# Score blocks without their masked quarter in a fused attention and FFN block, short tiles with their rows swapped

## The chip, the cores and the metric

One core of a Trainium2 chip. The metric is the device time of one execution in microseconds. TensorE (PE) does the matmuls, VectorE (DVE) reductions and elementwise work, ScalarE (ACT) activations and copies, GpSimd (POOL) elementwise work in SBUF, SyncE (SP) issues nearly all the DMAs.

## What is computed

The input x is 8 batches of 1024 rows of 256 numbers, fp32 throughout. The first half is causal self-attention with 16 heads of 64 and a bias that depends on the distance of key and query:

```python
bias = rel_table[clip(pos[None, :] - pos[:, None] + 16, 0, 32)]   # per head
q, k, v = x @ Wq, x @ Wk, x @ Wv                                   # per head, 64 columns
scores = q @ k.T / 8 + bias
scores = where(tril, scores, -inf)
out = softmax(scores) @ v
y = x + layernorm(concat(out) @ Wp + bp)     # x was normalised before q, k, v
```

The second half is a feed-forward block on the normalised y (a mix with the row before, a sigmoid gate, a squared relu), with a normalised residual again. Every distance of 16 or more into the past has the same bias, which softmax takes away; so the kernel adds the bias only in a band of 144 columns that ends with a tile's diagonal block, and sets the masked scores there to -1e30.

## The kernel before

**Units and tiles.** The work is cut in 64 units: 8 batches by 8 pairs of heads. The two heads of a pair lie on partitions 0-63 and 64-127 of q and k. A unit has 8 tiles of scores, tile tb being 128 queries (tb*128 on) against the (tb+1)*128 keys that they may see. Tiles 0 to 3 are *short* (128 to 512 keys), tiles 4 to 7 *long* (640 to 1024 keys). A unit goes in four steps, each with a long and a short tile: (7, 1), (6, 0), (5, 3), (4, 2) (STEPS, L21).

**A score tile, do_scores (L974).** A long tile is computed in two parts of half its keys, each in a PSUM tile "s" of two banks (ring "sl" of two, allocated from a pool, L411); the diagonal block is at the end of the second part. A short tile is one part, in two of four fixed PSUM banks "pm" (L377) that all other matmuls use too. A part is four matmuls (L1000): two query halves (output partitions 0-63 and 64-127) by two heads (contraction over partitions 0-63 and 64-127), each of 64x64 weights against all the part's keys. In the diagonal block, the first query half against the second 64 keys is wholly masked, and is computed all the same. Then, for the part that has the diagonal, DVE adds the band table bm (L1029); bm is one SBUF tile of 128 x 16 heads x 144. DVE takes the maximum (nmax, L1037), ACT the exponential into SBUF with its sum (p, L1057), POOL scales by the reciprocal sum (L1145).

**After it.** turn (L1156) transposes p in blocks of 32x32 on DVE (L1166), shuffle (L1219) moves the blocks to their partitions with 16 DMAs (L1226), and do_av (L1234, matmuls at L1252) multiplies by v into pm, two heads in the two column groups. save (L1269) copies the result to oT. project_out (L651) multiplies oT by Wp. Projections q, k, v (do_qk, do_v), project_out and the FFN use the helper matmul (L388), which splits the 128 output partitions in two matmuls of 64; their array shape is 128 rows by 64 columns, where the scores' is 64 by 64. Each fp32 matmul makes two records in the profile.

**The order of the work.** Every piece is a task that is handed to a Planner (L128) with an engine, an estimated cost, what it reads and writes, and a priority. The planner simulates the engines (L191) and writes each engine's instructions out in the order of the better of two simulations (run, L278). Matmul tasks have a mode: "rows" for scores, "cols" for all others. A change of mode is charged SWITCH = 0.09 us, and a task in the other mode has URGENT added to its rank when PE picks its next task (L216). RANK (L46) adds an offset per kind of task to the first simulation's priorities. The start of the kernel, up to the first tiles, is planned alone, without RANK (L1393). The band table is made at the start: a line per head is written to DRAM (skew, L1336) and read back skewed to bm (L1340).

Of the kernel before, what the change touches and what calls it, by code (L numbers as in the profile page):

```python
# [42 lines left out]
URGENT = 1.05  # L43
# [3 lines left out]
    "pe:part.go": -0.82,  # L47
    "dve:top.go": 1.9,
    "act:exp.go": -3.14,
    "dve:bias.go": 1.02,  # L50
    "pool:do_scores.behind": 6.53,
    "act:do_scores.<lambda>": -2.87,
    "pool:do_scores.both": 6.86,
    "dve:do_scores.<lambda>": -0.11,
    "pool:do_scores.<lambda>": -4.38,
    "pool:scale.go": 6.48,
    "dve:one.go": 1.8,
    "pe:do_qk.go": -0.33,
    "act:do_qk.<lambda>": -20.88,
    "sp:shuffle.move": 21.5,  # L60
    "pe:do_v.go": 0.57,
    "act:do_v.<lambda>": 11.6,
    "sp:load_wqk.go": -9.79,
    "sp:load_wv.go": 1.65,
    "pe:do_av.go": 0.22,
    "act:save.<lambda>": -6.41,
    "sp:load_rows.<lambda>": -6.4,
    "dve:norm_stats.go": 2.38,
    "pe:one.go": -0.19,
    "dve:one.plus_old": -14.51,  # L70
    "pool:normed.power": -0.11,
    "pool:normed.go": 6.49,
    "dve:by_dma.<lambda>": -1.51,
    "sp:by_dma.leave": -24.02,
    "sp:by_dma.<lambda>": -17.77,
    "act:by_dma.place": 4.69,
    "pool:plus.go": -26.3,
    "pool:s2.<lambda>": -47.14,
    "act:s3.go": 2.12,
    "dve:s4.go": 3.56,  # L80
    "pe:s5.go": 0.53,
    "act:s5.<lambda>": 17.56,
    "pool:s5.<lambda>": -0.97,
    "pe:second.go": -2.43,
    "act:s6.<lambda>": 22.56,
    "dve:s7.<lambda>": -5.69,
    "sp:s9.<lambda>": -14.9,
    "pe:some.go": 1.42,
    "act:normed.go_edge": -15,
# [18 lines left out]
class Ring:  # L108


    def __init__(self, pool, shape, tag, n):
        self.pool, self.shape, self.tag, self.n, self.owners = pool, shape, tag, n, []

# [14 lines left out]
class Planner:  # L128
# [149 lines left out]
    def run(self, rounds, urgent=1.0, rank={}):  # L278
# [25 lines left out]
        for t, _, _, seen in order:  # L304
            t.held = held.get(t, ())
            for b in t.makes:
                b.tile = b.ring.pool.tile(
                    b.ring.shape, F32, tag=b.ring.tag, name=b.name, bufs=b.ring.n
                )
                if b.view is not None:  # L310
                    b.tile = b.view(b.tile)
            t.fn()
            t.seen = seen
# [3 lines left out]
def tile_attn_ffn_block(  # L317
# [59 lines left out]
    bank = [ps_m.tile([P, HB], F32, name=f"pm{i}") for i in range(4)]  # L377
    plan = Planner(len(bank))
# [9 lines left out]
    def matmul(dst, lhs, rhs, first, last):  # L388
# [20 lines left out]
        "k": Ring(acts, [P, T], "k", 2),  # L409
        "v": Ring(acts, [P, NT, P], "v", 1),  # L410
        "sl": Ring(ps_l, [P, 2, HB], "sl", 2),  # L411
# [33 lines left out]
    def load_wqk(u, prio):  # L445

        pr = units[u][1]
        for name, w in (("q", Wq), ("k", Wk)):
            buf = weights[u, name] = R["w" + name](f"w{name}_{u}")

            def go(buf=buf, w=w):
                for cc in range(NC):
                    nc.sync.dma_start(
                        buf.tile[:, cc, :].rearrange("p (h d) -> p h d", d=D),
                        w[2 * pr : 2 * pr + 2, cc * P : (cc + 1) * P, :].rearrange(
                            "h p d -> p h d"
                        ),
                    )

            add("sp", 2 * ISSUE, go, w=[buf], prio=prio)  # L460

# [189 lines left out]
    def project_out(b, c, prs, prio):  # L651
# [6 lines left out]
        def one(k):  # L658
            def go():
                for pr in prs:  # L660
                    matmul(
                        pm(t)[:, :C],
                        oT[b, pr, c].tile[:, (1 - k) * P : (2 - k) * P],
                        wp_sb[:, pr, :],
                        (pr == prs[0]),
                        (pr == prs[-1]),
                    )
# [306 lines left out]
    def do_scores(u, tb, prio):  # L974


        n = (tb + 1) * P
        size = "long" if n > HB else "short"
        parts = [(0, n // 2), (n // 2, n)] if n > HB else [(0, n)]
# [7 lines left out]
        def part(i, c0, c1):  # L987

            sl = R["sl"](f"s_{what}_{i}") if size == "long" else None
            keep = [sl] if sl else []  # L990

# [3 lines left out]
            def go():  # L995
                for half in range(2):
                    for hh in range(2):
                        rows = slice(hh * D, (hh + 1) * D)
                        o = half * D
                        nc.tensor.matmul(  # L1000
                            s(hh)[o : o + D],
                            q.tile[rows, tb * P + o : tb * P + o + D],
                            k.tile[rows, c0:c1],
# [6 lines left out]
                0.05 + (c1 - c0) * 0.00169,  # L1010
# [11 lines left out]
            def bias(h0, h1):  # L1022
                def go():
                    if sl:
                        dst = sl.tile[:, :, c1 - c0 - w : c1 - c0]
                        src = bm[:, 2 * pr : 2 * pr + 2, BW - w :]
                    else:
                        dst, src = s(h0)[:, n - w : n], bm[:, 2 * pr + h0, BW - w :]
# [3 lines left out]
                done = add("dve", cost, go, t, bm_done, r=keep, prio=prio - 0.5)  # L1032
# [268 lines left out]
    with tc.tile_pool(name="prep", bufs=1) as prep:  # L1301
# [38 lines left out]
        bm_done = add("sp", ISSUE, lambda: nc.sync.dma_start(bm, moved), skew_done, prio=-4)  # L1340
        load_wv(0, -3)
# [21 lines left out]
        load_wqk(1, -1)  # L1363
        for half in range(2):
# [64 lines left out]
    for m in range(LAST):  # L1429
# [10 lines left out]
        if st == 3:  # L1440
            if u + 2 < NU:
                load_wqk(u + 2, m)
            do_v(u, 1, m + 0.3)
# [70 lines left out]
```

## Time and profile before

| | |
|---|---|
| median of 3 runs (lowest, highest) | 2208.03 us (2206.36, 2208.11) |
| profiled execution, its own time | 2206.46 us |
| its span, first to last instruction | 2204.7 us |
| granted TensorE clock, mean | 0.997 |
| ACT busy, POOL busy | 1412.6 us, 1524.2 us |
| PE and DVE busy from 30 to 2100 us | 2061.52 us, 1886.13 us |
| PE waits for another engine or a DMA, whole span | 22.3 us in 11 waits, 9.6 of them ahead of its first matmuls |
| DMA queue of SyncE | 272,144 packets, 384.87 MB, 72.1% of the 16 DMA engines' time |
| 1 shuffle DMA (d from blocks, 2032 of them) | 144 KB, 2.6 us from issue to landing |

Busy times are summed per engine over the execution; engines work side by side, so they do not add up to the span. A line of the timeline gives start, length, engine, source line, operation, output and inputs, shape and count. A matmul's start is recorded, and its end is modelled, so the lengths of neighbouring matmuls overlap; distances between starts are what can be trusted. "64*64" and "128*64" are the rows and columns of the array in use.

### The profile page before, as it was taken

How to read it: one execution, taken by the hardware profiler on the slowest of the kernel's cores; microseconds unless marked ns; L12 is line 12 of the kernel's file. 1: busy time of each engine (PE TensorE's matmuls, PEld its weight loads, DVE VectorE, ACT ScalarE, POOL GpSimd, SP SyncE). 2: the span in 40 equal slices, each digit the busy share in tenths (PEclk: the TensorE clock that was granted, in tenths of full speed). 3: DMA queues.
4: the chain of work that ended last, by engine and by line, in shares of the span. 5: the costliest groups of instructions: out<-in, count | busy, mean ns of one | idle time of the engine just before them, and what ended most of it. 6: DMA issues, size and time to landing. Idle time of an engine off the chain costs nothing.

```text
span 2204.7 us, 61232 instructions
## 1 busy us (share of the span) xinstructions
PE 2172.5 (99%) x21312; PEld 1175.2 (53%) x21312; DVE 1967.5 (89%) x4460; ACT 1412.6 (64%) x4314; POOL 1524.2 (69%) x3709
## 2 busy tenths in 40 slices
PE   7999999999999999999999999999999999999997
PEld 3455555555555545555555555555555555555565
DVE  5989999989999899998999889999898989999876
ACT  5666766657576676766667566666666656666554
POOL 4666677766777667776677757776677866677553
PEclk9999999999999999999999999999999999999999
DMA  5878877778777887777877787777777768777560
GB/s 159 188 179 204 197 176 173 173 192 194 184 168 174 195 192 173 173 172 194 190 177 173 168 205 191 176 173 170 196 186 174 180 167 214 180 183 180 128 160 25
DMA packets 272596, 388.92 MB, mean 176 GB/s; under 512 B 142624, under 2 KB 199968, under 8 KB 272160
## 3 DMA queue, kind: packets, MB, share of 16 engines
q1 hardware_dynamic: 272144, 384.87, 72.1%
q8 instruction: 170, 2.79, 0.5%
q14 instruction: 138, 1.13, 0.2%
q10 hardware_dynamic: 144, 0.14, 0.0%
HBM read 59.91 MB, written 25.29 MB: 39 GB/s over the span
## 4 chain that ended last, share of the span: by engine, by line
PE 92%; DVE 4%; DMA 1%; POOL 1%; ACT 1%; issue 0%; SPq 0%; ACTq 0%; DVEq 0%; POOLq 0%
PE pm L392 47%; PE pm L1252 22%; PE s L1000 16%; PE pm L1000 7%; DVE nmax L1037 1%; DVE blocks L1166 1%; DMA out_dram<-r 1%; DMA skew<-line 0%; DMA raw<-in_L_ffn_W_r_dram 0%; POOL p L1145 0%; ACT p L1057 0%; DVE pm L1029 0%; DVE xk L801 0%; DVE s L1029 0%; DMA tab<-in_L_attn_rel_table_dram 0%
## 5 line engine op out<-in xcount | busy, mean ns | idle before, releaser
L1145 POOL TENSOR_SCALAR p<-p,rcp 128x512 f32<-128x512 f32 (+5 forms) x1536 | 882.9, 591 | 108.7 <-DVE rcp L1124 77.1
L1057 ACT ACTIVATE p<-s,nmax 128x512 f32<-128x512 f32 (+3 forms) x1024 | 618.9, 607 | 416.2 <-DVE nmax L1037 320.2
L1166 DVE STREAM_TRANSPOSE blocks<-p 128x256 f32<-128x256 f32 (+1 forms) x1016 | 733.1, 754 | 46.1 <-POOL p L1145 38.3
L1037 DVE TENSOR_REDUCE nmax<-s 128x2 f32<-128x1024 f32 (+3 forms) x512 | 519.8, 1015 | 22.0 <-PE s L1000 18.1
L1252 PE MATMUL pm<-d,v 128*64 128x256 f32 (+1 forms) x5120 | 523.4, 359 | 0.0
L1252 PEld LDWEIGHTS pm<-d,v 128*64 128x64 f32 x5120 | 351.8, 137 | 217.9 <-issue 36.8
L1000 PE MATMUL s<-k,q 64*64 64x512 f32 (+3 forms) x4096 | 415.9, 517 | 5.6 <-ACT p L1057 5.4
L1057 ACT ACTIVATE p<-pm,nmax 128x256 f32<-128x256 f32 (+3 forms) x512 | 267.6, 525 | 144.2 <-DVE nmax L1037 104.1
L1000 PEld LDWEIGHTS s<-k,q 64*64 64x64 f32 x4096 | 142.4, 132 | 215.3 <-issue 98.4
L392 PE MATMUL pm<-wv,xnT 128*64 128x128 f32 x4096 | 248.0, 274 | 0.0
L392 PE MATMUL pm<-xnT,wq 128*64 128x512 f32 x1024 | 243.9, 597 | 2.6 <-ACT p L1057 2.6
L392 PEld LDWEIGHTS pm<-wv,xnT 128*64 128x64 f32 x4096 | 226.6, 137 | 36.6 <-ACT p L1057 14.1
L392 PE MATMUL pm<-xnT,wk 128*64 128x512 f32 x1024 | 245.2, 600 | 0.0
L392 PE MATMUL pm<-wp_sb,oT 128*64 128x256 f32 x2048 | 242.7, 383 | 0.7 <-ACT oT L1275 0.7
L1037 DVE TENSOR_REDUCE nmax<-pm 128x1 f32<-128x256 f32 (+3 forms) x512 | 235.0, 475 | 0.0
L1057 ACT ACTIVATION_READ_ACCUMULATOR p<-s,nmax 128x1 f32 x1024 | 203.3, 199 | 0.0
L392 PEld LDWEIGHTS pm<-wp_sb,oT 128*64 128x64 f32 x2048 | 139.7, 137 | 114.1 <-issue 40.3
L1029 DVE TENSOR_TENSOR pm<-pm,bm 128x144 f32<-128x144 f32 (+1 forms) x512 | 131.0, 301 | 72.1 <-PE pm L1000 69.7
L1000 PE MATMUL pm<-k,q 64*64 64x256 f32 (+3 forms) x2048 | 194.5, 450 | 0.4
L1114 POOL TENSOR_TENSOR tot<-tot,rcp 128x4 f32<-128x4 f32 x256 | 51.1, 200 | 161.6 <-ACT p L1057 97.4
L1133 POOL TENSOR_TENSOR rcp<-rcp,part 128x4 f32<-128x4 f32 x256 | 51.9, 203 | 131.5 <-DVE part L1124 110.9
L392 PEld LDWEIGHTS pm<-xnT,wq 128*64 128x64 f32 x1024 | 67.7, 136 | 119.0 <-issue 101.8
(103 smaller groups left out, 2231.9 us busy)
## 6 DMA issues: line engine op xcount, KB each, us to landing
d<-blocks SPq DMA_DIRECT2D x2032, 144.0 KB, 2.6
xin<-in_L_attn_x_dram SPq DMA_DIRECT2D x32, 256.0 KB, 2.9
wq<-in_L_attn_Wq_dram SPq DMA_DIRECT2D x128, 64.0 KB, 2.2
wk<-in_L_attn_Wk_dram SPq DMA_DIRECT2D x128, 64.0 KB, 2.3
wv<-in_L_attn_Wv_dram SPq DMA_DIRECT2D x64, 128.0 KB, 2.9
xre<-in_L_attn_x_dram SPq DMA_DIRECT2D x32, 256.0 KB, 2.9
out_dram<-r SPq DMA_DIRECT2D x32, 256.0 KB, 2.2
via_in<-st_in SPq DMA_DIRECT2D x112, 64.0 KB, 1.9
```

What stands on the lines that cost most here:

```text
L392: nc.tensor.matmul(dst[rows], lhs[:, rows], rhs, start=first, stop=last)
L1000: nc.tensor.matmul(s(hh)[o : o + D], q.tile[rows, tb * P + o : tb * P + o + D], k.tile[rows, c0:c1], start=True, stop=True,)
L1029: nc.vector.tensor_tensor(dst, dst, src, ALU.add)
L1037: nc.vector.tensor_reduce(nmax.tile[:, i, h0:h1], sl.tile[:, :, : c1 - c0] if sl else s(h0), AX.X, ALU.max, negate=True,)
L1057: nc.scalar.activation(ps[hh].tile[:, c0:c1], s(hh), AF.Exp, bias=nmax.tile[:, i, hh : hh + 1], scale=1.0, accum_out=tot.tile[:, i, hh : h ...
L1114: nc.gpsimd.tensor_tensor(tot.tile, tot.tile, rcp.tile, ALU.mult)
L1133: lambda: nc.gpsimd.tensor_tensor(rcp.tile, rcp.tile, inv.tile[:, 0:1, :].to_broadcast([P, 2, 2]), ALU.mult),
L1145: nc.gpsimd.tensor_scalar(p, p, rcp.tile[:, i, hh : hh + 1], 1.0, ALU.mult, ALU.mult)
L1166: nc.vector.transpose(blocks[g][:, :, s0 : s0 + 2 * tb + 1 : 2, hh, :].rearrange("p r a j -> p a r j"), p.tile[:, :n].rearrange("p (a r j) ...
L1252: nc.tensor.matmul(dst, v[:, jt, rows], src, start=(jt == 0), stop=(jt == 2 * k + 1),)
```

## The change

- In each tile, the two matmuls (one per head) of the query half that cannot see the last 64 keys leave these 64 columns out. The quarter of PSUM that they would have written keeps what was there; the band addition puts -1e30 on it, as on all masked scores.
- In short tiles the query halves are swapped: output partitions 0-63 hold the second half, 64-127 the first. So the narrower matmuls write partitions 0-63 in long tiles and 64-127 in short ones. Rows stay swapped through p, d and oT; project_out picks its slices of oT so that they come out in place.
- The band of a short tile needs its rows swapped too. It is loaded per unit from skew in DRAM into a ring of two tiles "bf", by two DMAs of 64 partitions, two units ahead.
- The two long score tiles become fixed PSUM tiles ("longs") and are cleared with the four banks by DVE at the start.
- The planner's cost of such a part is 32 columns lower. URGENT goes from 1.05 to 0.41 and all offsets of RANK change (most by a few units; the table is left out below).

```diff
-URGENT = 1.05
+URGENT = 0.41
...
+                if b.ring.fixed:
+                    b.tile = b.ring.fixed[b.ring.owners.index(b) % b.ring.n]
+                else:
...
+    longs = [ps_l.tile([P, 2, HB], F32, name=f"sl{i}") for i in range(2)]
+    for t in bank + longs:
+        nc.vector.memset(t, 0.0)
...
+        "bf": Ring(ins, [P, 2, BW], "bf", 2),
...
+    def load_bf(u, prio):
+
+        pr = units[u][1]
+        buf = bf[u] = R["bf"](f"bf_{u}")
+
+        def go():
+            for o in (0, D):
+                nc.sync.dma_start(
+                    buf.tile[D - o : P - o],
+                    bass.AP(
+                        tensor=skew.tensor,
+                        offset=skew.offset + 2 * pr * WL + P - 1 + o * (H * WL - 1),
+                        ap=[[H * WL - 1, D], [WL, 2], [1, BW]],
+                    ),
+                )
+
+        add("sp", 2 * ISSUE, go, skew_done, w=[buf], prio=prio, mb=0.15)
...
 def project_out
-                    matmul(
-                        pm(t)[:, :C],
-                        oT[b, pr, c].tile[:, (1 - k) * P : (2 - k) * P],
-                        wp_sb[:, pr, :],
-                        (pr == prs[0]),
-                        (pr == prs[-1]),
-                    )
+                    for o in (0, D):
+                        at = (1 - k) * P + (D - o if c < NCP // 2 else o)
+                        nc.tensor.matmul(
+                            pm(t)[o : o + D, :C],
+                            oT[b, pr, c].tile[:, at : at + D],
+                            wp_sb[:, pr, :],
+                            start=(pr == prs[0]),
+                            stop=(pr == prs[-1]),
+                        )
...
 def do_scores
+        flipped = size == "short"
...
-                for half in range(2):
+                for o in (0, D):
+                    at = D - o if flipped else o
+                    end = c1 - D if c1 == n and at == 0 else c1
                     for hh in range(2):
                         rows = slice(hh * D, (hh + 1) * D)
-                        o = half * D
                         nc.tensor.matmul(
-                            s(hh)[o : o + D],
-                            q.tile[rows, tb * P + o : tb * P + o + D],
-                            k.tile[rows, c0:c1],
+                            s(hh)[o : o + D, : end - c0],
+                            q.tile[rows, tb * P + at : tb * P + at + D],
+                            k.tile[rows, c0:end],
...
-                0.05 + (c1 - c0) * 0.00169,
+                0.05 + (c1 - c0 - (D / 2 if c1 == n else 0)) * 0.00169,
...
-                        dst, src = s(h0)[:, n - w : n], bm[:, 2 * pr + h0, BW - w :]
+                        dst, src = s(h0)[:, n - w : n], bf[u].tile[:, h0, BW - w :]
...
+        load_bf(0, -3.5)
...
+        load_bf(1, -0.5)
...
                 load_wqk(u + 2, m)
+                load_bf(u + 2, m)
```

## The prediction

> **What bounds the kernel now.** I read the page's busy shares first, then the chain that ended last, then the TensorE timeline, because the change touches the shape of TensorE's instructions.
>
> ```profile
> PE 2172.5 (99%) x21312; PEld 1175.2 (53%) x21312; DVE 1967.5 (89%) x4460; ACT 1412.6 (64%) x4314; POOL 1524.2 (69%) x3709
> ...
> PE 92%; DVE 4%; DMA 1%; POOL 1%; ACT 1%; issue 0%; SPq 0%; ACTq 0%; DVEq 0%; POOLq 0%
> ```
>
> TensorE (PE) is busy for 99% of the span and makes 92% of the chain. The table of stretches gives PE 2061.52 us of the 2070 us between 30 and 2100 us: only 8.5 us without a matmul. So time taken off PE is time taken off the kernel, until another engine holds it up; VectorE (DVE) is next, 1886.13 of the same 2070 us (91%).
>
> How PE spends a score block is seen by asking the PE timeline for windows so short that only one set of instructions starts in each:
>
> ```profile
> 995.63 0.28 PE L1252 MATMUL pm<-d,v 128*64 128x128 f32 x2
> ...
> 995.84 0.55 PE L1000 MATMUL pm<-k,q 64*64 64x384 f32 x4
> ...
> 996.21 0.50 PE L1000 MATMUL pm<-k,q 64*64 64x384 f32 x4
> ...
> 996.53 0.45 PE L1000 MATMUL s<-k,q 64*64 64x320 f32 x4
> ...
> 997.34 0.45 PE L1000 MATMUL s<-k,q 64*64 64x320 f32 x4
> ...
> 997.72 0.44 PE L392 MATMUL pm<-wp_sb,oT 128*64 128x256 f32 x2
> ```
>
> The first column is the start, the second a modelled length (overlapping, not to be added). A part of a score tile is 4 matmuls, and it makes 8 records: two passes each. The passes start four at a time: two heads (array rows 0-63 and 64-127) by two column groups (query halves, output partitions 0-63 and 64-127), all inside a 0.04 us window. Three things follow.
>
> 1. *Price of a column.* From 996.53 to 997.34 lie three sets of 320 columns: 0.27 us each, 0.844 ns per column and pass. 64 columns less in two passes are 2 x 64 x 0.844 = 0.108 us, for the column group that has them less.
> 2. *Order.* Two passes of one matmul use the same quarter of the array, so the first four records must be first passes of four different matmuls. The second to fourth matmul then began before the first one's second pass: a quarter that is free does not wait for its neighbour's turn.
> 3. *Switch of array shape.* 995.63 to 995.84 is 0.21 us for a pass of 128 columns (0.108): 0.10 over. 997.34 to 997.72 is 0.38 for 0.27: 0.11 over. The first pass after a switch also costs 0.37 instead of 0.324: 0.05 over. One stay in 64*64 shape thus costs 0.26 us beyond its columns. Between sets of one shape nothing of this size appears.
>
> Now what stands together in one stay:
>
> ```profile
> 1205.42 0.45 PE L1000 MATMUL pm<-k,q 64*64 64x128 f32 x8
> 1205.80 1.94 PE L392 MATMUL pm<-xnT,wk 128*64 128x512 f32 x8
> 1207.67 1.73 PE L1000 MATMUL s<-k,q 64*64 64x448 f32 x16
> ...
> 1224.48 0.88 PE L1000 MATMUL pm<-k,q 64*64 64x384 f32 x8
> 1225.17 1.26 PE L1000 MATMUL s<-k,q 64*64 64x320 f32 x16
> 1226.36 1.94 PE L392 MATMUL pm<-xnT,wq 128*64 128x512 f32 x8
> ...
> 1233.40 0.66 PE L1000 MATMUL pm<-k,q 64*64 64x256 f32 x8
> 1233.97 1.09 PE L1000 MATMUL s<-k,q 64*64 64x512 f32 x8
> 1234.98 1.95 PE L392 MATMUL pm<-wvT,ka 128*64 128x256 f32 x16
> 1236.86 1.09 PE L1000 MATMUL s<-k,q 64*64 64x512 f32 x8
> ```
>
> At 1224.48 a short tile (output pm) and both parts of a long one (output s, x16) stand together. At 1205.42 and 1207.67 each stands alone. At 1233.40 a short tile has the long tile's first part only, and the second part, the one with the masked quarter, is alone at 1236.86. Counted so over the whole timeline there are 328 stays; 182 hold a short tile and a second part of a long one, in 141 of them the short tile first, in 41 the long one.
>
> **The change, part by part.**
>
> *Narrower matmuls.* 64 units of 8 tiles: in each tile one column group has 64 columns less, in a long tile the first group, in a short (flipped) tile the second. One group alone gains nothing if the other is waited for, and a stay in one shape ends when both are done. A stay that holds both kinds is shortened in both groups, by 0.108 us. A stay with one kind is shortened in one group only; whether that lead survives the switch is not in the trace of before, since there both groups always carry equal work. Ends: 182 x 0.108 = 19.7 us if a switch waits for both groups, 256 x 0.108 = 27.6 us if the lead is carried through (256 pairs of tiles). The nearest row is the extra 0.10 us at every switch, which looks like an array that is emptied first; I take 19.7 us.
>
> The Trainium skill bears on this from two sides. "TensorEngine Tiling (Array Packing)", Key Properties, says that changing the tiling mode drains the TensorE; that would give the 19.7. "TensorE: Matmul & The Clock Gate", Part 3, What overlaps and what doesn't, says that matmuls start and end in strict program order; the four starts at 995.84 do not agree, and by that rule the gain would be the 4.4 us of the rival below.
>
> *Bias for short tiles from DRAM.* 64 units x 2 DMAs of 64 partitions with 2 pieces of 576 B: 16,384 packets. The queue's 272,144 packets took 72.1% of 16 x 2204.7 us, 93 ns each; so 1.5 ms of 16 engines, 4.3% of their time. 72% becomes at most 76%, and the load is made two units (some 69 us) ahead: nothing on the path. Issue: SyncE shows 0.92 us for two weight loads (1009.68, L453), so 0.9 us more per unit of 34.4, in which two shuffles take 2 x 10.6. What is queued behind it on SyncE are the shuffles (L1226), which do_av needs; matmuls waited for a shuffle's landing only 5.7 us in all. I take 0; the upper end is one delay of 0.9 us per unit on some, say 10 us, kept for the range.
>
> *Bias addition and maximum.* Same shapes (128x144, 306 ns; 128x288, 452 ns), other source: 0.
>
> *Fixed score tiles, memsets.* DVE gets six memsets, 4096 columns in all, at the very start. Nearest row:
>
> ```profile
> L1037 DVE TENSOR_REDUCE nmax<-s 128x2 f32<-128x1024 f32 x128 | 155.8, 1217 | 1.0
> ```
>
> 1.19 ns per column: 4.9 us from about 0.7, so until 5.6. DVE's first instruction now starts at 4.88, and its first statistics at 5.43 lead to PE's start at 8.43. Late by 0 (if the memsets are faster) to 0.8 us. Four more DMAs on SyncE before and after 17 us (0.45 each) may make the weights that PE waits for at 25.10 (1.28 us) up to 1.8 us later. Together 0 to 2.6; I take 1.0. Reusing a fixed score tile waits for the same exponentials as before: 0.
>
> *project_out.* The same 2 matmuls of 64x256 per block, other slices: 0.
>
> *New ranks, and URGENT 0.41 for 1.05.* They set the order that the planner writes out, so which tiles share a stay and how many stays there are. No row prices this; each stay more or less is 0.26 us, and 0.37 if it breaks or makes a pair. The stays are bounded by 256 pairs kept whole (72 less: -19 us for the switches, and up to -8 more for the 74 pairs then made) and by the parts' number, 768 (far above). I take 0, as the middle row is the order now, and keep 30 either way, 8 to 11 us.
>
> *What is late next.* DVE's share of the main stretch goes from 91 to 92%. ScalarE already waits 424 us for maxima (nmax L1037), and banks come free behind it; a PE that is 1% faster may meet this more often than in the 8.5 us it idles now.
>
> Sum against the profiled execution's 2206.46 us: 2206.46 - 19.7 + 1.0 = 2187.8. The median of the runs shown is 1.57 above that execution: 2189.3, so **2189 us**, 0.9% faster.
>
> **The rivals.**
>
> *A lead is carried through switches.* For: the quarters seem to run on their own. Against: the 0.10 us at each switch. 2208.03 - 27.6 + 1.0 = 2181.
>
> *Strict order: the change does not do what it says.* If a matmul may not start before the one ahead of it in the program, the second group's early end in a short tile is lost, for the next tile's first group must start first; only the long-before-short stays gain, 41 x 0.108 = 4.4 us: 2204.6. Against: the four starts.
>
> *Vector work gives half back.* For: 91% in the main stretch. Against: 8.5 us idle only. 10 us back: 2199.
>
> *More stays: slower.* URGENT is what a change of array shape counts against a task's lateness; with 0.41 the planner may leave a shape for a slightly later task, as at 1234.98, where one tile is cut in two stays. Each such cut costs 0.26 + 0.108 = 0.37 us. It decides from 18.7 / 0.37 = 51 more stays (379) on; 72 more (400) give 2189.3 + 26.6 = 2216. For: the value and all ranks move at once. Against: the planner keeps the better of two simulated orders, and both charge each switch.
>
> **How the numbers follow.** The forecast 47% (2181 to 2198: ends of the start, of the stays and of the DMA); lead carried 14%; half given back 10%; strict order 12%; more stays 17%. About 0.2% (4.4 us) is what a measurement of this kernel can tell from no change. Faster by more than that (below 2203.6): 47 + 14 + 10 + 4 of the strict case = 75%. Within: 8 of the strict case and 1 of the stays = 9%. Slower: 16%. The range goes from 2174 (lead carried and 27 stays fewer: 2181 - 7) to 2210, which leaves out the slower case and little else.
>
> **What would show it.** Right: matmuls of 64x448, 64x384, 64x320, 64x256 and so on beside the full ones in L1000; inside a stay that holds both kinds, starts of the two column groups drift apart by about 0.05 us per pass and meet again, and the stay is 0.11 us shorter; stays near 328; PE still over 98%. Lead carried: after a lone long tile the two groups of the next 128*64 matmuls start 0.1 us apart instead of together. Strict: no such drift after a short tile. Wrong as a whole: over 380 stays, or PE idle well above 10 us in the middle, with DVE as the releaser, or shuffles landing late.

## The result, and the profile after

| | before | after |
|---|---|---|
| median (lowest, highest) | 2208.11 us (2206.36, 2209.07; 5 runs) | 2215.43 us (2214.47, 2217.14; 5 runs) |
| ratio to before, 95% interval | | 1.0035 [1.0024, 1.0046] |
| profiled execution, its span | 2206.46, 2204.7 us | 2215.31, 2213.5 us |
| PE busy from 30 to 2100 us | 2061.52 | 2053.32 |
| DVE busy, whole span | 1967.5 | 2023.0 |

The kernel became 0.35% slower; the forecast was 0.9% faster. First the page of the kernel after, busy shares and chain:

```profile
PE 2172.5 (98%) x21312; PEld 1201.0 (54%) x21312; DVE 2023.0 (91%) x4466; ACT 1424.0 (64%) x4314; POOL 1524.2 (69%) x3709
...
PE 80%; DVE 12%; ACT 3%; DMA 2%; issue 2%; POOL 1%; SPq 0%; DVEq 0%; ACTq 0%; POOLq 0%
```

DVE has six instructions more (the memsets, 3.8 us together) and yet is busy for 55.5 us more; its share of the chain went from 4% to 12%. That is the first hint: the change's text has nothing on VectorE but another source of the same additions.

Does TensorE do what the change says? The PE timeline of the kernel after, first one stay whole, then windows so short that only a few first records lie in each (start, modelled length, shape, count). A row also counts the records that are still running when its window opens, so what starts in a window is what the count grows by:

```profile
1009.36 1.09 PE L1037 MATMUL sl<-k,q 64*64 64x512 f32 x8
1010.27 0.60 PE L1037 MATMUL pm<-k,q 64*64 64x256 f32 x8
1010.61 1.02 PE L1037 MATMUL sl<-k,q 64*64 64x512 f32 x8
1011.57 0.44 PE L692 MATMUL pm<-wp_sb,oT 128*64 128x256 f32 x2
...
1010.27 0.38 PE L1037 MATMUL pm<-k,q 64*64 64x256 f32 x4
...
1010.27 0.51 PE L1037 MATMUL pm<-k,q 64*64 64x256 f32 x6
...
1010.27 0.60 PE L1037 MATMUL pm<-k,q 64*64 64x256 f32 x8
...
1010.61 0.59 PE L1037 MATMUL sl<-k,q 64*64 64x512 f32 x2
...
1010.61 0.64 PE L1037 MATMUL sl<-k,q 64*64 64x512 f32 x4
```

The windows are 1010.27 (all four first passes of the short tile), 1010.44 to 1010.46 (two more records: the narrower group starts its second pass at 1010.45), 1010.485 to 1010.50 (the other group, 0.04 us later), 1010.60 to 1010.62 (the narrower group is already in the next long part, at 1010.61) and 1010.70 to 1010.715 (the other group follows at 1010.705, 0.09 us later). The first group's next matmul stands ahead of the second group's in the program and starts after it. So the two column groups drift apart and meet again; the stay takes 2.21 us, from 1009.36 to 1011.57, where one with the same parts took 2.31 before:

```profile
1003.04 0.66 PE L1000 MATMUL pm<-k,q 64*64 64x256 f32 x8
1003.52 1.90 PE L1000 MATMUL s<-k,q 64*64 64x512 f32 x16
1005.35 1.95 PE L392 MATMUL pm<-wp_sb,oT 128*64 128x256 f32 x16
```

The mechanism of the forecast is there. (The Trainium skill, "TensorE: Matmul & The Clock Gate", Part 3, What overlaps and what doesn't, says that matmuls start and end in strict program order; the starts at 1010.61 and 1010.705 stand the other way round, so that does not hold for these matmuls in different quarters.)

So where did the time come from? I added up the records of the trace: for every stay (matmuls in 64*64 shape with no other shape among them), the time from its first start to the first start after it, and the time between stays, from the first matmul on. What follows the last stay is left out (61 to 62 us, 66 in e15). A pair is a narrowed short tile and a narrowed long part in one stay; the expectation of e1 counts one less for the kernel after. All times in us, one profiled execution each; the experiments' kernels are explained below.

| kernel | stays | pairs | in stays | between | sum |
|---|---|---|---|---|---|
| before | 328 | 182 | 559.3 | 1565.8 | 2125.1 |
| after | 352 | 158 | 560.8 | 1572.9 | 2133.7 |
| e1, after at full width | 352 | | 572.9 | 1570.4 | 2143.3 |
| e2, after with the bias additions together | 352 | 158 | 547.9 | 1571.1 | 2119.0 |
| e12, e2 without the loads | 352 | 158 | 549.0 | 1570.1 | 2119.1 |
| e6, order of before, no loads | 328 | 182 | 541.5 | 1568.5 | 2110.0 |
| e10, order of before, with the loads | 328 | 182 | 548.7 | 1577.2 | 2125.9 |
| e7, before with the bias additions apart | 328 | 182 | 566.4 | 1603.8 | 2170.2 |
| e13, e10 with one load per unit | 328 | 182 | 545.7 | 1574.1 | 2119.8 |
| e14, planner repriced | 315 | 195 | 551.7 | 1569.1 | 2120.8 |
| e15, planner repriced, other offsets | 311 | 175 | 543.5 | 1573.1 | 2116.6 |

After, the columns of the busier group in the stays fall from 491.5 to 474.7 us (158 pairs of 0.107; by the records' distances, 0.269 us for a pass of 320 columns and 0.429 for one of 512, a column of a pass costs 0.833 ns), and the stays still take 1.5 us longer. Between them 7.1 us are added. Where in the stays? Those that begin a long tile (its first part, with a short tile): 42 instead of 23, and the median time beyond their columns went from 0.171 to 0.396 us; the stays of all three parts kept 0.176. The waits view of PE says for what; the line of after (us in total, times, longest; 5.4 us in 4 waits before):

```profile
PE sl L1037 <- ACT p L1094: 14.3, 22, 3.9
```

PE waits for a score tile to be read by the exponential, which waits for the maximum, which is DVE's. The waits count only stretches with no matmul at all; a stay in which one quarter still runs while the others stand does not show there.

What changed on DVE is seen in its timeline around one short tile of 256 keys and two heads. Before:

```profile
1003.99 0.50 DVE L1029 TENSOR_TENSOR pm<-pm,bm 128x144 f32<-128x144 f32 x2
...
1004.46 0.40 DVE L1037 TENSOR_REDUCE nmax<-pm 128x1 f32<-128x256 f32 x1
```

and after:

```profile
900.58 0.28 DVE L1066 TENSOR_TENSOR pm<-pm,bf 128x144 f32<-128x144 f32 x1
900.90 0.42 DVE L1074 TENSOR_REDUCE nmax<-pm 128x1 f32<-128x256 f32 x1
901.24 0.30 DVE L1066 TENSOR_TENSOR pm<-pm,bf 128x144 f32<-128x144 f32 x1
901.58 0.42 DVE L1074 TENSOR_REDUCE nmax<-pm 128x1 f32<-128x256 f32 x1
901.92 1.21 DVE L1074 TENSOR_REDUCE nmax<-sl 128x2 f32<-128x1024 f32 x1
```

Before, the two additions follow each other (x2: 0.50 us for both). After, each maximum stands directly behind the addition that it needs and starts 0.32 to 0.34 us behind that one's start; the four take 900.58 to 901.92, 1.34 us. Over the whole trace two additions of short tiles are neighbours 253 times before and once after; such an addition followed at once by a short tile's maximum occurs 114 and 472 times. The 114 do not need that addition: where it has 144 columns, they start 0.21 us behind its start (median), 0.09 us before it ends. The 472 start 0.34 us behind it (0.32 us behind one of 128 columns), 0.03 us after its end. So the two kinds differ by what the maximum waits for and not by which operations are neighbours. The source of this order is RANK: the offsets of the maximum and the addition, dve:top and dve:bias, were 1.9 and 1.02, so the second head's addition came ahead of the first head's maximum; now they are 1.15 and 1.79, the other way round.

### The profile page after: what moved, and what is told of

It reads as the page before. It is cut to its first block, busy times and chain, and to the rows that moved or that the text cites. A ratio compares the mean times of both kernels' runs of the same rounds, so it can differ in the third digit from the quotient of the medians.

```text
span 2213.5 us, 61461 instructions
## 1 busy us (share of the span) xinstructions
PE 2172.5 (98%) x21312; PEld 1201.0 (54%) x21312; DVE 2023.0 (91%) x4466; ACT 1424.0 (64%) x4314; POOL 1524.2 (69%) x3709
## 3 DMA queue, kind: packets, MB, share of 16 engines
q14 instruction: 140, 1.15, 0.2%
## 4 chain that ended last, share of the span: by engine, by line
PE 80%; DVE 12%; ACT 3%; DMA 2%; issue 2%; POOL 1%; SPq 0%; DVEq 0%; ACTq 0%; POOLq 0%
PE pm L400 33%; PE pm L1289 19%; PE sl L1037 15%; PE pm L692 9%; PE pm L1037 6%; DVE nmax L1074 4%; DVE blocks L1203 3%; ACT p L1094 2%; DVE sl L1066 1%; DVE pm L1066 1%; DVE xr L832 1%; DMA wq<-in_L_attn_Wq_dram 0%; DMA wk<-in_L_attn_Wk_dram 0%; POOL p L1182 0%; DMA skew<-line 0%
## 5 line engine op out<-in xcount | busy, mean ns | idle before, releaser
L1094 ACT ACTIVATE p<-sl,nmax 128x512 f32<-128x512 f32 (+3 forms) x1024 | 617.9, 606 | 435.8 <-DVE nmax L1074 267.8
L1074 DVE TENSOR_REDUCE nmax<-sl 128x2 f32<-128x1024 f32 (+3 forms) x512 | 520.2, 1016 | 19.0 <-PE sl L1037 8.2
L1037 PE MATMUL sl<-k,q 64*64 64x384 f32 (+4 forms) x4096 | 421.5, 506 | 14.9 <-ACT p L1094 14.3
L1037 PEld LDWEIGHTS sl<-k,q 64*64 64x64 f32 x4096 | 164.3, 132 | 203.0 <-ACT p L1094 95.9
L1074 DVE TENSOR_REDUCE nmax<-pm 128x1 f32<-128x256 f32 (+3 forms) x512 | 250.9, 490 | 16.2
L1094 ACT ACTIVATION_READ_ACCUMULATOR p<-sl,nmax 128x1 f32 x1024 | 201.2, 196 | 0.0
L1037 PE MATMUL pm<-k,q 64*64 64x448 f32 (+7 forms) x2048 | 192.4, 424 | 0.0
L1066 DVE TENSOR_TENSOR pm<-pm,bf 128x144 f32<-128x144 f32 (+1 forms) x512 | 151.6, 296 | 42.7 <-PE pm L1037 41.3
L1136 POOL TENSOR_TENSOR rcp<-nmax 128x2 f32<-128x2 f32 x256 | 53.1, 207 | 169.8 <-DVE nmax L1074 87.8
```

Of the source, the lines that this page charges most:

```text
L1037: nc.tensor.matmul(s(hh)[o : o + D, : end - c0], q.tile[rows, tb * P + at : tb * P + at + D], k.tile[rows, c0:end], start=True, stop=True,)
L1066: nc.vector.tensor_tensor(dst, dst, src, ALU.add)
L1074: nc.vector.tensor_reduce(nmax.tile[:, i, h0:h1], sl.tile[:, :, : c1 - c0] if sl else s(h0), AX.X, ALU.max, negate=True,)
L1094: nc.scalar.activation(ps[hh].tile[:, c0:c1], s(hh), AF.Exp, bias=nmax.tile[:, i, hh : hh + 1], scale=1.0, accum_out=tot.tile[:, i, hh : h ...
L1136: nc.gpsimd.tensor_tensor(rcp.tile[:, 0, :], m1, m0, ALU.subtract)
```

## The experiments

The theories: **VectorE's order** (the new offsets make each maximum wait for its own addition), **the loads** (the bias DMAs hold up what SyncE issues behind them), **more stays** (352 for 328, fewer pairs), and against all three **the matmuls** (narrowing gains nothing, or fixed tiles cost). The expectations call the first A, the second D, the third B and the fourth C; E is the case that fixed tiles or memsets cost. Ratios are to the kernel before on the same chip, with 95% intervals.

**e1: the matmuls at full width, all else as after.**

```diff
-                    end = c1 - D if c1 == n and at == 0 else c1
+                    end = c1
```

> The changed kernel with its order of instructions kept, but with all score matmuls at full width again (the flip, the bias from DRAM and the memsets stay). In the changed kernel's records 157 stays in 64*64 shape hold a short tile and a long tile's second part; at 0.107 us each the narrower matmuls are worth 16.8 us there. Theory A (the narrowing pays; VectorE's new order, in which each maximum directly follows the bias addition that it depends on, takes it back) and theory B (the narrowing pays; PE's own new order, with more stays and fewer pairs, takes it back) expect 2215 + 10 to 17 = 2225 to 2232. Theory C (the narrower matmuls gain nothing here, or what comes with them costs) expects 2215 or less.

2226.01 us, 1.0076 [1.0064, 1.0088]. So narrowing is worth about 9 us in the order of after (1.0076 against 1.0035; 9.6 by the table's sums), and the rest of the change costs 17 us against before. By the table the narrower parts saved 12.1 of their 16.8 us in the stays and gave 2.5 back between them.

**e2: the second head's addition directly behind the first's, all else as after.** The order is planned as it was, and a pass behind the planner moves the instruction.

```diff
+def twins_together(order):
+    second = {t.twin: (i, row) for i, row in enumerate(order) for t in row[:1] if hasattr(t, "twin")}
+    out, gone = [], set()
+    for i, row in enumerate(order):
+        if row[0] in gone:
+            continue
+        out.append(row)
+        if row[0] in second and second[row[0]][0] > i:
+            out.append(second[row[0]][1])
+            gone.add(second[row[0]][1][0])
+    return out
...
+        order = twins_together(order)
...
+                if h0 == 1:
+                    done.twin = ready[0]
```

> The changed kernel with one thing moved in VectorE's order: the second head's bias addition of a short tile goes directly behind the first head's, ahead of the first maximum, as it mostly stood before. Nothing is moved on the other engines. Theory A expects VectorE's busy time to fall from 2023 by some 30 us and most of the 24 us of long PE stalls to go: 2192 to 2203. Theory B expects PE to be where it was: 2211 to 2217. Theory C likewise 2211 to 2217.

2201.88 us, 0.9969 [0.9957, 0.9980]: by the ratios 14.6 us less than after, with the same instructions, stays and loads, and now faster than before. Its page:

```profile
PE 2162.4 (98%) x21312; PEld 1203.9 (55%) x21312; DVE 1983.5 (90%) x4466; ACT 1410.9 (64%) x4314; POOL 1526.1 (69%) x3709
...
PE 94%; DVE 3%; DMA 1%; issue 1%; ACT 1%; SPq 0%; POOL 0%; ACTq 0%; DVEq 0%; POOLq 0%
```

and DVE's timeline at the same short tile:

```profile
893.60 0.50 DVE L1080 TENSOR_TENSOR pm<-pm,bf 128x144 f32<-128x144 f32 x2
894.01 0.74 DVE L1090 TENSOR_REDUCE nmax<-pm 128x1 f32<-128x256 f32 x2
894.69 1.23 DVE L1090 TENSOR_REDUCE nmax<-sl 128x2 f32<-128x1024 f32 x1
```

From 893.60 to 894.69 the four take 1.09 us instead of 1.34. 256 such tiles of 0.25 us would be 64 us of DVE; its busy time, which does not hold the short gaps ahead of a waiting maximum, fell by 39.5. Its share of the chain is back at 3%. The 14.7 us that the sums of the table lose between after and e2 lie almost all in the stays (12.9).

**e7: the reverse, in the kernel before.** Addition, maximum, addition, maximum for each short tile, one behind the other.

```diff
+def fours_together(order):
+    rows = {row[0]: row for row in order}
+    out, gone = [], set()
+    for row in order:
+        if row[0] in gone:
+            continue
+        four = getattr(row[0], "four", None) or [row[0]]
+        for t in four:
+            out.append(rows[t])
+            gone.add(t)
+    return out
...
+                done.four = None if sl else four
+                if not sl:
+                    four.append(done)
```

> The kernel before, with VectorE's order alone changed: each short tile's four instructions stand together as in the changed kernel, bias, maximum, bias, maximum, so that each maximum directly follows the addition it depends on. Theory A (this order costs VectorE some 0.1 us per pair and PE then waits for score tiles) expects VectorE's busy time up by 25 to 40 us and the time at 2215 to 2230. If the gain in the run with the biases together came from something else, 2206 to 2211.

2248.84 us, 1.0191 [1.0177, 1.0205]: 41 us slower by an order alone, with no narrowing, flipping or load in it, and above the 2215 to 2230 expected.

```profile
PE 2182.3 (97%) x21312; PEld 1173.9 (52%) x21312; DVE 2026.6 (90%) x4460; ACT 1391.8 (62%) x4314; POOL 1527.2 (68%) x3709
...
PE 76%; DVE 16%; ACT 4%; issue 2%; DMA 1%; POOL 1%; SPq 0%; DVEq 0%; ACTq 0%; POOLq 0%
```

DVE's busy time, 2026.6, is that of after (2023.0). The loss is nearly three times the 14.6 us, and most of it lies between the stays (1603.8 for 1565.8). The pass moves instructions behind the planner's back, where after was planned in its order; that this is the whole of the difference was not tested. So e7 shows that the order of these four can cost that much, and e2 is what sizes it for this change.

**e3, e4, e10: the code of after in the order of before.** Offsets, URGENT and the parts' costs of before; the bias DMAs are issued with k's weights, so the planner plans as before.

```diff
-URGENT = 0.41
+URGENT = 1.05
...
-                0.05 + (c1 - c0 - (D / 2 if c1 == n else 0)) * 0.00169,
+                0.05 + (c1 - c0) * 0.00169,
...
+            if name == "k" and u >= 2:
+                more = [bf.setdefault(u, R["bf"](f"bf_{u}"))]
...
+                weights_in()
+                for m in more:
+                    bf_move(m, pr)
```

e3 and e4 have this with the weight load's function renamed, by which its offset drops out (329 stays); e4 is e3 at full width. In e10 the name is kept and the order is that of before (328 stays).

> Narrow matmuls, flipped short tiles, bias from DRAM (ring of three, its two DMAs issued with the load of wk), fixed score tiles, but the ranks, URGENT and costs of before, so that the planned order is that of before but for a few places (327 stays planned, 181 of them pairs, where before had 326 and 182). Theories A and B (the narrowing pays where pairs share a stay) expect 2208 - 181 x 0.107 + 1 = 2190, between 2187 and 2197 if some is lost to waits. Theory C expects 2206 or more.

> The kernel of the run before it with full-width score matmuls: it has the flip, the bias from DRAM, the fixed tiles and the memsets alone, in the order of before. Theories A and B expect 2208 to 2211 (the start 1 to 2 us later). Theory C, in the form that what comes with the narrowing costs, expects 2215 or more.

> Like the run with narrow matmuls in the order of before, with a flaw of that run mended: there the task that loads wq and wk had lost its rank with its function's name, so that SyncE's order was not that of before. Here all planned orders are those of before; the two bias loads per unit are issued right behind the load of wk. If the loads themselves cost what that run lost against the run without loads (2209 against 2190), this is 2204 to 2210. If the lost rank cost it, 2190 to 2196.

e3: 2209.08 us, 0.9993 [0.9983, 1.0004]. e4: 2214.8, 1.0030 [1.0019, 1.0040]. e10: 2208.02, 0.9989 [0.9978, 0.9999]. Old order and all 182 pairs, and yet hardly a gain, where A and B had 2187 to 2197 for e3: VectorE's order is not the whole cause. The times of e3 and e10 also scatter more than most (e10 2200.22 to 2211.94 in 11 runs).

**e6: the order of before without the loads.** The short tiles take their bias from bm, with its rows as they are there; the loads and the swap of the band's rows are left out.

```diff
-                        dst, src = s(h0)[:, n - w : n], bf[u].tile[:, h0, BW - w :]
+                        dst, src = s(h0)[:, n - w : n], bm[:, 2 * pr + h0, BW - w :]
```

> The kernel with narrow matmuls and flipped short tiles in the order of before, without the bias loads per unit: short tiles take their bias from the table in SBUF, whose rows are not flipped, so their bias and mask stand on the wrong rows. Everything else has the work of the full kernel. Theory D (the narrowing pays by its pairs, and the loads on SyncE take most of it back) expects 2208 + 1 - 182 x 0.107 = 2189 to 2195. Theory E expects 2200 or more. If the order of before simply cannot use a faster PE, 2203 to 2209.

2190.46 us, 0.9924 [0.9910, 0.9937]: this is the forecast's gain (17.1 of 18.7 us), and the loads in the order of before cost 0.0065 of the time, 14 us. How, is read from the queues and waits. SyncE's queue before, and then in e10:

```profile
1025.24 0.94 SPq L453 DMA_DIRECT2D wk<-in_L_attn_Wk_dram  x2
1026.23 0.46 SPq L467 DMA_DIRECT2D wv<-in_L_attn_Wv_dram  x1
1026.87 0.37 SPq L602 DMA_DIRECT2D xn<-via_in  x1
```

```profile
1030.02 0.94 SPq L474 DMA_DIRECT2D wk<-in_L_attn_Wk_dram  x2
1031.01 1.31 SPq L457 DMA_DIRECT2D bf<-skew  x2
1032.36 0.59 SPq L499 DMA_DIRECT2D wv<-in_L_attn_Wv_dram  x1
1033.06 0.44 SPq L634 DMA_DIRECT2D xn<-via_in  x1
```

The two bias loads hold SyncE from 1031.01 to 1032.36, and xn is issued behind them. ScalarE waits for xn in its own queue, with exponentials behind it. The waits of ACT for xn and yn, in e6 (yn 2.7 us more) and in e10:

```profile
ACT xnT L621 <- DMA xn<-via_in: 33.9, 19, 3.4
```

```profile
ACT xnT L646 <- DMA xn<-via_in: 61.6, 28, 4.9
ACT ynT L646 <- DMA yn<-via_y: 15.7, 10, 2.4
```

Together 40.7 us more of waiting on ScalarE. On PE, the time without a matmul from 30 to 2100 us is 20.4 us in e10 and 10.4 in e6, with new waits for ScalarE's copies of q and k (5.5 us together), and its wait for the FFN's first weights at the start is 3.9 us for 0.9. Its weight loads wait 9.2 us for shuffles, 5.7 in e6. That xn's delay makes these waits is read from the order of the queue; no run moves xn alone. In the kernel after, where the planner knew of the loads, the same wait is short, and shorter than before (38.0):

```profile
ACT xnT L643 <- DMA xn<-via_in: 7.3, 8, 1.6
```

**e12: e2 without the loads.** The twin pass of e2; the load tasks stay in the plan and issue nothing; bias as in e6.

```diff
-            for o in (0, D):
-                nc.sync.dma_start(
...
+            pass
```

> The changed kernel's planned order with the bias additions together (2201.9), without the bias loads: their tasks stay in the plan but issue nothing, and short tiles take their bias from the unflipped table, so bias and mask stand on the wrong rows. In the changed kernel the planner gave the loads their own place and cost. My account of that run (2208 - 16.8 for 157 pairs + 9.1 for 24 more stays + 1) leaves at most 2 us for the loads: 2199 to 2202. If loads cost there what they cost in the order of before, 2184 to 2197.

2199.21 us, 0.9955 [0.9943, 0.9968], against e2's 0.9969 [0.9957, 0.9980]: the intervals overlap, and the sums of the table are alike (2119.1, 2119.0). In the changed plan the loads cost some 3 us or nothing.

**e5: only the fixed long tiles and the memsets, in the kernel before.**

```diff
+    longs = [ps_l.tile([P, 2, HB], F32, name=f"sl{i}") for i in range(2)]
+    for t in bank + longs:
+        nc.vector.memset(t, 0.0)
...
-        "sl": Ring(ps_l, [P, 2, HB], "sl", 2),
+        "sl": Ring(ps_l, [P, 2, HB], "sl", 2, longs),
```

> The kernel before with only the fixed long score tiles and the six memsets of PSUM at the start; its planned order is unchanged. The run with everything but the narrowing, in the order of before, was 5.5 us slower than before. If the 128 bias loads on SyncE cost that (theory D), this one stays at 2208 to 2210. If the fixed tiles or the memsets cost it (theory E: other waits on reuse), it is at 2212 to 2216.

2206.73 us, 0.9996 [0.9987, 1.0005]: no cost that can be measured.

**e8: the loads on ScalarE's queue**, behind its copy of v, in the order of before.

```diff
+        def copy():
+            nc.scalar.copy(dst.tile[:, g * n : (g + 1) * n, :], view())
+            for m in more:
+                bf_move(m, units[u + 2][1], nc.scalar)
```

> The run before this one, with the bias loads issued by ScalarE, behind its copy of the second half of v, and not by SyncE; same packets, same sizes, all planned orders those of before. If SyncE's issue time is what the loads cost (shuffles and the norm's transposes through DRAM are issued later and ScalarE waits for them), this is 2190 to 2197. If the packets themselves cost it, the same as with SyncE. If ScalarE's own 0.9 us of issue per unit costs as much, 2200 to 2210.

2314.65 us, 1.0482 [1.0464, 1.0501]: 106 us slower, with 124 DMAs on ScalarE, 0.86 us each; 2190 to 2210 was expected. ScalarE's timeline in e8:

```profile
1036.06 0.59 ACT L993 COPY v<-pm 128x512 f32<-128x512 f32 x1 [0.30 <-PE pm L399]
1036.06 1.33 ACTq L457 DMA_DIRECT2D bf<-skew  x2
1037.44 0.20 ACT L1147 ACTIVATE rcp<-rcp 128x4 f32<-128x4 f32 x1 [0.80 <-POOL p L1185]
```

The issue lasts as long as on SyncE (1.33 us for two), and the next activation starts only behind it, at 1037.44 (no later activation starts before the end of such an issue in any of the 62 units, and in 39 of them one starts 0.05 us after it); ScalarE stands in the middle of the chain from maximum to exponential. ScalarE's wait for xn rose as well, to 111.4 us in 28 waits. Part of the 106 us may be the clock: the granted clock was 0.984 here and 0.997 before. 1.6% of 2311.8 us against 0.3% of 2204.7 makes some 30 us, an estimate of the most that the clock can have cost. A plain miss as a cure.

**e9 and e13: one load per unit.** A flipped table is made once in DRAM, and a unit's band comes by one DMA of 128 pieces of 1152 B; order of before. In e9 the table is made at the start, in e13 behind the weights, with the first two units loaded as in e10. The edit shown is against e10.

```diff
     def bf_move(buf, pr):
-        for o in (0, D):
-            nc.sync.dma_start(
...
+        nc.sync.dma_start(buf.tile.rearrange("p h w -> p (h w)"), flip[pr])
...
+            for o in (0, D):
+                for h in range(2):
+                    nc.sync.dma_start(
+                        flip[:, D - o : P - o, h * BW : (h + 1) * BW].rearrange("k p w -> p k w"),
```

> All planned orders those of before, loads on SyncE, but one per unit in place of two: 128 pieces of 1152 B from a flipped copy of the table that is written to DRAM at the start by four more DMAs. If issue time or packets cost, the loss is halved: about midway between the run with two loads and 2190, plus up to 2 us at the start.

> The run with one bias load per unit, in the order of before, with its start mended: there PE waited 10.6 us at the start for weights behind the four DMAs that build the flipped table (1.3 before). Here units 0 and 1 are loaded from the line table and the flipped table is built behind the weights. If SyncE's issue time (and what is issued behind it) is what the loads cost in this order, half of it gives half of the 17.5 us: 2197 to 2201, and the earlier run's 2204 minus 9 agrees. If the loads cost by their number of packets or bytes at the memory side rather than by issue time, the same halving of packets cannot be told apart; if neither, 2204 to 2208.

e9: 2204.34 us, 0.9982 [0.9974, 0.9991], with a new wait of PE at the start:

```profile
PE pm L399 <- DMA raw<-in_L_ffn_W_r_dram: 10.6, 1, 10.6
```

(1.3 us before): the four DMAs that make the table hold up the FFN's weights. e13: 2198.26 us, 0.9959 [0.9946, 0.9971]. A load's issue takes SyncE 0.47 us instead of 2 x 0.63 (medians of e13 and e10), and about half of what the loads cost in the order of before is won back (e6 has 0.9924, e10 0.9989). The packets are halved with it, so this run does not tell issue time from their number.

**e14 and e15: the planner told what the chip showed.** The planner simulates its order; its own end is 2205.1 us for before and 2183.0 for after, so by its model the change gains 22. Its model gives every narrowed part half of the saving, paired or not, charges 0.09 for a switch, and knows no wait between neighbouring instructions of DVE. e14 charges 0.185, gives 0.107 to a pair alone, makes one task of a short tile's two additions, and has offsets found anew by this model; e15 has other offsets, with fewer stays.

```diff
-SWITCH = 0.09
+SWITCH = 0.185
...
-            end = free[e] = start + t.cost
+            end = start + t.cost
+            if t.side and lead == -t.side:
+                end -= 0.107
+                lead = 0
+            elif t.side:
+                lead = t.side
+            free[e] = end
...
             else:
+                bias(0, 2)
                 for hh in range(2):
-                    bias(hh, hh + 1)
                     exp(hh, top(hh, hh + 1))
```

> The changed kernel with the planner's prices as the runs showed them (a switch 0.185 us each way, a lone narrow part gains nothing, a pair gains 0.107 us, one task for both bias additions of a short tile), and URGENT and offsets searched anew in the planner's own simulation. Its plan has 313 stays and 195 pairs (the changed kernel 350 and 158, before 326 and 182). By the account, 2208 - 195 x 0.107 - 13 x 0.38 + 1 + 3 for the loads = 2186 if no new waits come, 2186 to 2200 with some. If the loss of the changed kernel lies in something that this account lacks, 2200 or more.

> Like the run before it, another set of offsets from the same search: 309 stays planned, 175 pairs. By the account 2208 - 175 x 0.107 - 17 x 0.38 + 1 + 3 = 2187 if no new waits come; its simulated end is 4 us later than the other's, so 2187 to 2204.

e14: 2203.22 us, 0.9978 [0.9969, 0.9987]; e15: 2199.39, 0.9959 [0.9945, 0.9972]. Both are faster than before and after. e15 lies within its 2187 to 2204, and e14 is above its 2186 to 2200: it has the most pairs (195), and its stays take longer than those of e6 (551.7, 541.5). A line of its waits:

```profile
PE sl L1046 <- ACT p L1106: 20.3, 19, 4.2
```

The order with more in a stay waits more for a free score tile; DVE makes 15% of its chain. What in the planner's model is missing for that is open. e13 and e15 are the fastest of the kernels that leave nothing out, about 0.4% faster than before and 0.8% faster than after.

**The sum.** e6, e12, e2 and after form a ladder from before, one step at a time:

| step | ratio | step, us (of 2208) | the same by the table's sums |
|---|---|---|---|
| before to e6: narrowing, flipping, fixed tiles | 0.9924 | -16.8 | -15.1 |
| to e12: new order but for the neighbours on DVE; 24 stays more, 24 pairs fewer | 0.9955 | +6.8 | +9.1 |
| to e2: the loads, as planned | 0.9969 | +3.1 | -0.1 |
| to after: each maximum behind its own addition | 1.0035 | +14.6 | +14.7 |

Each ratio is uncertain by about 0.0012, so a step by some 4 us: the first, the second and the last step are clear of that, the loads' 3 us are not, nor which of the first and the last is larger. The second step changes every engine's order at once; that stays and pairs are what costs there is worked out from the sums, and no run changes them alone. The steps also hang on each other, so the sizes are those of this path: narrowing is worth 17 us here, 9 in the order of after (e1), and 8 in the order of before with the loads (e3 against e4).

## Why the prediction was wrong

The sign was wrong. By the prediction's own steps:

- **Narrower matmuls: right.** 0.108 us a pair was forecast; 0.107 is what the records give. The choice of 19.7 over 27.6 us was right too: a lone long tile's stay ends no earlier than before (0.171 us beyond the busier group's columns before and after; a lone short tile's 0.166 and 0.153), and the two first matmuls behind it start 0.007 us apart, as before, where a carried lead would have shown 0.1; so a lead is lost at the switch. With 182 pairs in the order of before and without the loads (e6) the gain was 17.1 us; forecast 18.7. In the order of after it was 9, which the step, having no order in it, did not foresee. The rivals "lead carried" and "strict order" fall: the first by the lone stays, the second by the starts at 1010.61 and 1010.705. The four starts at 995.84, which the prediction set against strict order, could stand in the program's order themselves; that choice was right on thin evidence.
- **Fixed score tiles, memsets, project_out: right** (e5: 0.9996; PE's first matmul came 0.3 us later).
- **"Bias addition and maximum. Same shapes ... other source: 0": the first failing step, with the next.** Shapes and durations did stay; what the step left out is that an instruction's price on DVE hangs on its neighbour. A pair of independent additions takes 0.50 us where one takes 0.31; a maximum directly behind its own addition starts 0.34 us after it, one behind another addition 0.21 us. The row for the cheap case was in the profile of before: x2 in 0.50 us at 1003.99.
- **"New ranks, and URGENT 0.41 for 1.05 ... I take 0": the step that turned the sign.** It priced the ranks by what they set on TensorE, the number of stays. That part lay within what it kept: 24 more stays of the 30 kept for the range, and if the sums from e6 to e12 are put down to stays and pairs, (7.5 + 1.6 - 24 x 0.107) / 24 = 0.27 us a stay, for 0.26 forecast; with the 24 pairs 6.8 to 9.1 us, for the 8 to 11 kept. But RANK also orders DVE's instructions, and its two lines on dve:top and dve:bias swapped places: 14.6 us (e2), and 41 us in another plan (e7). The table of offsets was part of the change and was not read for that.
- **Loads: 0 forecast, 10 us kept as the upper end.** In the order of before, which this step spoke of, they cost 14 us (e10 against e6), over the end kept. The shuffles behind them, which the step named, account for 3.5 us of PE's waits; what grew most is ScalarE's wait for xn, whose transfer stood behind the weight loads in the profile of before too (1026.87), and the issue took 1.31 us per unit, not 0.9. In the plan of after they cost 3 us or nothing (e12 against e2): there the planner knew of them and gave them places of their own.
- **What is late next: right in kind, too small.** PE's idle time from 30 to 2100 us went from 8.5 to 16.7 us, released by the exponentials, as feared. The rival "vector work gives half back" had 10 us; 14.6 went there, but it argued from DVE's share of the time, not from its order, so that its size is near is luck.
- **The rival "more stays" forecast 2216 for 400 stays.** The time was that, the stays were 352. The price came mostly from DVE's order; so that rival is not confirmed by having its number.

The mechanism that was named first works; three costs in what came with it (6.8, 3.1 and 14.6 us) add up to 24.5 us on the ladder and outweigh it. Without the last of them the change would have gained (e2, 0.9969).

## What to carry to other kernels

Read a change of priorities on every engine that they order, and look in the trace for the pairs of neighbours that it makes or breaks: the same instructions cost 14.6 us more with each reduction directly behind its own producer. Price a DMA also by its issue on the queue that issues it, and look for who waits in order for what stands behind it; where the planner knows of the load, it may cost nothing, where it is put into a finished order, 14 us. Test a saving in the old order first: e6 would have shown what the matmuls give, apart from the new order.

## What the runs showed of the hardware

- Quarters of the array run ahead of each other by some 0.1 us inside a stay, out of program order (0.09 us at 1010.61), and behind a switch of array shape they start together again (0.007 us apart behind a lone long tile).
- On VectorE a second, independent addition of 128x144 starts 0.22 us behind the first (0.31 us long; median of before), a dependent maximum 0.34 us behind. For two additions and two maxima the difference is 0.25 us. The Trainium skill, "VectorE: DVE Perf Modes", Two Vector instructions with no wait between them, says that a held instruction starts only when every earlier one on VectorE has finished. It tells which are held by the partitions at which operands start, not by whose result is waited for, so it describes a neighbouring case; here the maximum that waits for the addition starts 0.03 us after its end.
- A DMA of 64 partitions with two pieces of 576 B holds the queue that issues it for 0.63 us on SyncE (e10) and 0.62 on ScalarE (e8), one of 128 pieces of 1152 B for 0.47 us (e13), by the median length of the issue.
